# A four-layer graph network on one core: the last layer's attentions for two batches at once, with the own score as shift and the mask as a factor

## The chip, the cores and the metric

The kernel runs on one core of one Trainium2 chip. The metric is the device time of one execution in microseconds (us). Every kernel here was profiled once, and timed against runs of the kernel before in the same rounds on the same chip.

Engine names: PE is TensorE (matmuls), PEld its weight loads, DVE is VectorE, ACT ScalarE, POOL GpSimd. `L567` in a profile line is line 567 of that kernel's source; the numbers differ between kernels, so the text says what each line is.

## The reference, cut to what matters

Four graph layers over one adjacency matrix, each followed by a residual layer norm. Layers 0 to 2 are almost untouched by the change. Layer 3 is this:

```python
# x: [8, 2048, 64] float32; graph: [2048, 2048], ~0.4% ones, symmetric, ones on the diagonal
NEG = -1e+16
def _gat_layer(h, mask, b):
    scores = jnp.einsum('...nd,...md->...nm', h, h)
    scores = jnp.where(mask, scores, NEG)
    attn = jax.nn.softmax(scores, axis=-1)
    return jnp.einsum('...nm,...md->...nd', attn, h) + b
mask = graph + jnp.eye(N) > 0
h = jnp.einsum('bnc,hdc->bhnd', x, Wh)               # 4 heads of 64
out_h = _gat_layer(h, mask[None, None], bh[None, :, None, :])
cat = jnp.transpose(out_h, (0, 2, 1, 3)).reshape(B, N, H * D)
z = jax.nn.leaky_relu(cat, negative_slope=0.2)
h2 = jnp.einsum('bnk,dk->bnd', z, Wo)
out2 = _gat_layer(h2, mask[None], bo)                # the "second attention"
z2 = jax.nn.leaky_relu(out2, negative_slope=0.2)
out = layernorm(z2) * gamma + beta                   # then layernorm(x + out)
```

There are 8 batches with five attentions each (four heads and the second one), and each attention is a full 2048 x 2048 table of weights in fp32.

## The kernel before

Weights are made transposed: 128 source nodes on the partitions, 512 target nodes on the free axis. Such a block is called a **step**; 16 steps make a **chunk** of 512 targets, and 4 chunks an attention. For each attention `prepare` first finds the masked row maxima of the scores in bf16 (the shift of the softmax), and `attend` then makes weights and sums.

```python
def prepare(u, b, h):
    ...
        # 16 small products: h with nodes on partitions
        nc.tensor.matmul(ph[:, q], state["xT"][k * D:(k + 1) * D, ts],
                         WhT[k * D:(k + 1) * D, h * D:(h + 1) * D], start=True, stop=True)
    ...
    for it in range(NT):                 # row maxima, 64 blocks of 128 x 512
        for c in range(NCH):
            nc.tensor.matmul(pa, hb[:, it * P:(it + 1) * P], hb[:, cs], start=True, stop=False)
            nc.tensor.matmul(pa, neg_id_bf, M[:, it, cs], start=False, stop=True)
            nc.vector.tensor_reduce(mx[:, it, c:c + 1], pa, AX.X, ALU.max)
    ...                                  # maxima transposed into row 64 of hm

def attend(u, b, h):
    for c in range(NCH):
        for jt in range(NT):
            pscore = ps_s.tile([P, CW], F32, name="pscore")          # 3 buffers
            nc.tensor.matmul(pscore, neg_id_bf, MT[:, jt, cs], start=True, stop=False)   # the mask
            nc.tensor.matmul(pscore, hs[:, jt * P:(jt + 1) * P], hm[:, cs], start=False, stop=True)
            w = wk.tile([P, CW], F32, name="w", bufs=3)
            nc.scalar.activation(w, pscore, AF.Exp)
            nc.tensor.matmul(po, hones[...], w, start=(jt == 0), stop=(jt == NT - 1))  # [h | 1]
        rec = wk.tile([D, CW], F32, name="rec", bufs=1)
        nc.vector.reciprocal(rec, po[(1 - hk) * D:(2 - hk) * D])
        ...                              # times the numerators, bias, leaky relu, product with Wo
```

## Time and profile before

| | before |
|---|---|
| time | 9961.3 us (median of 3; 9961.0 to 9972.2) |
| layers 0 to 2 and set-up, to the first score of layer 3 | 2162 us |
| layer 3's attentions | 7769 us, TensorE busy 99% |
| one step (one batch) | 2.015 us, 2560 of them |

To read the profile: the page gives the busy time of each engine and, in 40 slices, its busy share in tenths. `PEclk` is the TensorE clock that the throttle granted, in tenths. A group line gives line, engine, operation, output <- input with shapes, count, then total busy us and the mean ns of one, then the idle time of the engine just before these instructions and what ended it. A timeline line gives start, time taken (us), engine, line, operation, output <- input, shapes, and how many records are merged in it (x4); in brackets stands the idle time before it. Matmuls overlap in the pipeline, so TensorE's pace is read from **starts** in the timeline, not from durations. A fp32 product appears as two matmul records, two **passes**. I call the 0.43 us between starts of two dense passes of 512 columns a **slot**.

### The profile page before, as it was taken

The numbers are of one execution on the slowest core, as the hardware profiler recorded it, in microseconds if no ns is written. First come the engines' busy times: TensorE is split into PE (matmuls) and PEld (weight loads), VectorE is DVE, ScalarE is ACT, GpSimd is POOL, SyncE is SP. The second block draws the span as 40 slices with busy tenths as digits, with TensorE's granted clock in tenths as the row PEclk, the third lists the DMA queues.
The fourth block names the chain that finished last, engine by engine and source line by source line (L and its number), as shares of the span: only waits on it lengthen the run. The fifth ranks groups of instructions, "written<-read, shape, count | busy, mean of one in ns | idle before, by whom it ended". The sixth has DMA issues, their size and how long they took to land. (4 is left out here: it accounts for less than half of the span.)

```text
span 9967.4 us, 62454 instructions
## 1 busy us (share of the span) xinstructions
PE 9215.5 (92%) x24992; PEld 3477.5 (35%) x24992; DVE 4228.1 (42%) x5463; ACT 1870.1 (19%) x3156; POOL 597.4 (6%) x471
## 2 busy tenths in 40 slices
PE   3786698679999999999999999999999999999998
PEld 2332244223333333333333333333333333333332
DVE  6899423454334333433443343334333433243423
ACT  1000200012212221222122212221222122212221
POOL 4100301310000000000000000000000000000000
PEclk6898799869989998999899989997999899989997
DMA  2000000000000000000000000000000000000000
GB/s 86 0 0 1 0 0 1 0 1 0 0 0 3 0 0 0 3 0 0 0 3 0 0 0 3 0 0 0 2 0 0 0 3 0 0 0 3 0 0 2
DMA packets 43381, 29.87 MB, mean 3 GB/s; under 512 B 40977, under 2 KB 41041, under 8 KB 41041
## 3 DMA queue, kind: packets, MB, share of 16 engines
q1 hardware_dynamic: 26448, 21.68, 0.7%
q10 hardware_dynamic: 16640, 4.20, 0.2%
q8 instruction: 195, 3.19, 0.1%
q14 instruction: 98, 0.79, 0.0%
HBM read 21.68 MB, written 4.19 MB: 3 GB/s over the span
## 5 line engine op out<-in xcount | busy, mean ns | idle before, releaser
L565 PE MATMUL po<-w,hones 128*128 128x512 f32 x5120 | 2656.5, 622 | 2.1 <-ACT w L564 2.1
L562 PE MATMUL pscore<-hm,hs 65*128 65x512 f32 x5120 | 2650.8, 598 | 0.0
L564 ACT ACTIVATE w<-pscore 128x512 f32<-128x512 f32 x2560 | 1528.6, 597 | 5867.9 <-PE pscore L562 5867.9
L542 DVE TENSOR_REDUCE mx<-pa 128x1 f32<-128x512 f32 x2560 | 1720.9, 691 | 1220.2 <-PE pa L541 1219.2
L567 DVE RECIPROCAL rec<-po 64x512 f32<-64x512 f32 x160 | 536.6, 3353 | 2864.2 <-PE po L565 2864.2
L565 PEld LDWEIGHTS po<-w,hones 128*128 128x128 f32 x5120 | 880.2, 191 | 1245.8 <-ACT w L564 1161.0
L562 PEld LDWEIGHTS pscore<-hm,hs 65*128 65x128 f32 x5120 | 984.7, 193 | 758.1 <-issue 630.7
L540 PE MATMUL pa<-hb 64*128 64x512 bf16 x2560 | 1119.5, 437 | 33.7 <-DVE hb L533 17.2
L541 PE MATMUL pa<-M,neg_id_bf 128*128 128x512 fp8e4 x2560 | 1126.7, 440 | 0.0
L561 PE MATMUL pscore<-MT,neg_id_bf 128*128 128x512 fp8e4 x2560 | 974.8, 382 | 0.2 <-ACT M L458 0.2
L540 PEld LDWEIGHTS <-hb 64*128 64x128 bf16 x2560 | 242.4, 95 | 1299.2 <-issue 1281.3
L270 PE MATMUL acc<-w,H 128*128 128x512 f32 x1024 | 489.1, 632 | 54.0 <-DVE w L267 53.2
L541 PEld LDWEIGHTS <-neg_id_bf 128*128 128x128 bf16 x2560 | 249.6, 97 | 738.6 <-issue 738.6
L534 POOL COPY hm<-hs 64x512 f32<-64x512 f32 x160 | 110.3, 691 | 6234.9 <-ACT hs L532 6234.9
L368 PE MATMUL pa<-R,A 128*128 128x512 f32 x1024 | 453.4, 599 | 9.7 <-POOL R L359 9.3
L561 PEld LDWEIGHTS <-neg_id_bf 128*128 128x128 bf16 x2560 | 249.1, 97 | 474.3 <-issue 469.1
L270 PEld LDWEIGHTS acc<-w,H 128*128 128x128 f32 x1024 | 198.7, 201 | 339.3 <-issue 204.3
L267 DVE SCALAR_TENSOR_TENSOR w<-MT,w 128x1024 f32<-128x1024 fp8e4 x256 | 302.1, 1215 | 0.4
L160 POOL TENSOR_TENSOR ln_rstd<-ln_var,mhalf 128x16 f32<-128x16 f32 (+1 forms) x21 | 151.0, 7189 | 2450.2 <-DVE ln_var L157 2450.2
L368 PEld LDWEIGHTS pa<-R,A 128*128 128x128 f32 x1024 | 191.3, 190 | 269.1 <-issue 245.9
L416 PE MATMUL pa<-Y,A 128*128 128x512 f32 x512 | 219.9, 592 | 0.0
L549 DVE COPY hm<-pm 1x512 f32<-1x512 f32 x160 | 109.0, 682 | 248.4 <-PE pm L548 248.4
(184 smaller groups left out, 3891.9 us busy)
## 6 DMA issues: line engine op xcount, KB each, us to landing
at<-in_adj SPq DMA_DIRECT2D x16, 1024.0 KB, 5.2
X<-in_x ACTq DMA_DIRECT2D x16, 256.0 KB, 7.8
out<-O SPq DMA_DIRECT2D x8, 512.0 KB, 3.8
wt<-in_L_gnn_Wh SPq DMA_DIRECT2D x4, 32.0 KB, 4.6
wo<-in_L_gnn_Wo SPq DMA_DIRECT2D x1, 64.0 KB, 6.0
a<-in_L_gnn_a SPq DMA_DIRECT2D x2, 32.0 KB, 2.9
g<-in_L_gnn_ln_gamma SPq DMA_DIRECT2D x2, 32.0 KB, 2.9
b<-in_L_gnn_ln_beta SPq DMA_DIRECT2D x2, 32.0 KB, 3.1
```

The lines of the kernel that those rows point to most:

```text
L267: nc.vector.scalar_tensor_tensor(w, MT[:, jt, ih * HW:(ih + 1) * HW], 0.0, w, op0=ALU.is_equal, op1=ALU.mult)
L270: nc.tensor.matmul(acc[c], H[:, jt, p, k:k + 2, :].rearrange("p a d -> p (a d)"), w[:, c * CW:(c + 1) * CW], start=(jt == 0), stop=False)
L368: nc.tensor.matmul(pof, A[:, jt], R[:, jt, h].rearrange("p a f -> p (a f)"), start=(jt == 0), stop=False)
L416: nc.tensor.matmul(po, A[:, jt], Y[:, jt], start=(jt == 0), stop=(jt == NT - 1))
L540: nc.tensor.matmul(pa, hb[:, it * P:(it + 1) * P], hb[:, cs], start=True, stop=False)
L541: nc.tensor.matmul(pa, neg_id_bf, M[:, it, cs], start=False, stop=True)
L542: nc.vector.tensor_reduce(mx[:, it, c:c + 1], pa, AX.X, ALU.max)
L561: nc.tensor.matmul(pscore, neg_id_bf, MT[:, jt, cs], start=True, stop=False)
L562: nc.tensor.matmul(pscore, hs[:, jt * P:(jt + 1) * P], hm[:, cs], start=False, stop=True)
L564: nc.scalar.activation(w, pscore, AF.Exp)
L565: nc.tensor.matmul(po, hones[:, jt, hp, hk:hk + 2, :].rearrange("p a d -> p (a d)"), w, start=(jt == 0), stop=(jt == NT - 1))
L567: nc.vector.reciprocal(rec, po[(1 - hk) * D:(2 - hk) * D])
```

## The change

Its intent is to make layer 3 cheaper in five ways at once:

- Two batches lie on the two halves of the partitions. A head's score products use 64 rows each and its sums 64 columns each, so the two batches' products can run on halves of the array at once.
- The shift of the softmax is the node's own score, not the row maximum: the pass of maxima falls away. The shift rides in the place of feature 0 of `U`.
- The mask is a factor (VectorE multiplies the weights by 0 or 1), not a product that adds minus infinity.
- Features of a layer-normed node add up to zero, so feature 0 is redundant in the heads. Its place in `Xo` holds ones, and the sums of the weights come out there: no separate ones. The second attention has no redundant feature and pays two more products with ones.
- If a denominator is out of range, a flag is set and the old layer 3 runs after all.

The core of the diff, with cuts marked (layers 0 and 1 only use the mask as a factor, or copy it, instead of comparing):

```diff
+    W_SELF = 20.0
+        ps_s = l3.enter_context(tc.tile_pool(name="f3pss", bufs=2, space=PSUM))
+        ps_o = l3.enter_context(tc.tile_pool(name="f3pso", bufs=2, space=PSUM))
+        ps_m = l3.enter_context(tc.tile_pool(name="f3psm", bufs=2, space=PSUM))
...
+        def prepare(p, h, c):
...
+            pu = misc([P, CW])
+            nc.tensor.matmul(pu, G[:, h], xT[:, cs], start=True, stop=True)
+            nc.scalar.copy(U[:, cs], pu)
+            V = wk.tile([P, CW], BF16, name="V")
+            nc.gpsimd.tensor_tensor(V, xT[:, cs], U[:, cs], ALU.mult)
+            pv = misc([P, CW])
+            nc.tensor.matmul(pv, minus, V, start=True, stop=True)
+            nc.vector.tensor_tensor(U[:, cs], pv, U[:, cs], ALU.add)
...
+        def attend(p, h, c):
...
+            for jt in range(NT):
+                pscore = ps_s.tile([P, 2, CW], F32, name="pscore")
+                for k in range(2):
+                    half = slice(k * D, (k + 1) * D)
+                    nc.tensor.matmul(pscore[:, k], left[half, jt * P:(jt + 1) * P], right[half, cs], start=True, stop=True)
+                w = wk.tile([P, 2, CW], F32, name="w", bufs=4)
+                nc.scalar.activation(w, pscore, AF.Exp, bias=bias)
+                edge = ET[:, jt, cs].unsqueeze(1).to_broadcast([P, 2, CW])
+                nc.vector.scalar_tensor_tensor(w, w, 3.0e38, edge, op0=ALU.min, op1=ALU.mult)
+                for k in range(2):
+                    half = slice(k * D, (k + 1) * D)
+                    nc.tensor.matmul(po[half], rhs[:, jt, k], w[:, k], start=(jt == 0), stop=(jt == NT - 1))
+                if h == HN:
+                    for k in range(2):
+                        half = slice(k * D, (k + 1) * D)
+                        nc.tensor.matmul(pden[half], ones_d, w[:, k], start=(jt == 0), stop=(jt == NT - 1))
...
+            if h < HN:
...
+                nc.scalar.copy(o, po)
...
+                nc.tensor.matmul(pden, first, o, start=True, stop=True)
...
+                nc.tensor.matmul(pn, AT[:, h], o, start=True, stop=True)
+                nc.vector.reciprocal(rec, pden)
+                nc.vector.tensor_tensor(z, pn, rec, ALU.mult)
...
+                nc.tensor.matmul(ph, WoT[:, h], z, start=True, stop=True)
...
+        bad = nc.values_load(flag[0:1, 0:1], min_val=0, max_val=P * NP * (HN + 1) * NCH)
+    with tc.If(bad > 0), ExitStack() as l3:
...      the old layer 3
```

A step of the new kernel covers two batches, so there are 1024 steps in heads and 256 in second attentions.

## The prediction

> **What bounds the kernel now.** I read the table of engines first, then the strip of slices, then the three stretches (layers 0 to 2, layer 3, the end), then the groups of instructions kept apart by shape, and last the timeline of six microseconds inside an attention.
>
> The page, busy time and the two rows of TensorE:
>
> ```profile
> PE 9215.5 (92%) x24992; PEld 3477.5 (35%) x24992; DVE 4228.1 (42%) x5463; ACT 1870.1 (19%) x3156; POOL 597.4 (6%) x471
> ...
> PE   3786698679999999999999999999999999999998
> ...
> PEclk6898799869989998999899989997999899989997
> ```
>
> TensorE is busy from slice 9 on and nothing else comes near. The small dips of its clock recur once per batch. The stretches say where layer 3 lies (columns: busy us and count of PE, PEld, DVE, ACT, POOL, then the granted clock):
>
> ```profile
> 0.00:2162.00 2162.00, 1533.96 (x4139) 686.59 (x4139) 1319.64 (x1591) 216.24 (x364) 382.38 (x259) 0.82 0.04 10
> 2162.00:9931.00 7769.00, 7679.74 (x20850) 2790.16 (x20848) 2894.16 (x3850) 1651.60 (x2788) 201.59 (x205) 0.94 0.00 1
> ```
>
> From the first score at 2162 us to the last weighted sum at 9931 us, 7769 us, TensorE is busy 99%. The change is almost wholly in that stretch. The groups say what it is made of:
>
> ```profile
> L565 PE MATMUL po<-w,hones 128*128 128x512 f32 x5120 | 2656.5, 622 | 2.1 <-ACT w L564 2.1
> L562 PE MATMUL pscore<-hm,hs 65*128 65x512 f32 x5120 | 2650.8, 598 | 0.0
> L564 ACT ACTIVATE w<-pscore 128x512 f32<-128x512 f32 x2560 | 1528.6, 597 | 5867.9 <-PE pscore L562 5867.9
> L542 DVE TENSOR_REDUCE mx<-pa 128x1 f32<-128x512 f32 x2560 | 1720.9, 691 | 1220.2 <-PE pa L541 1219.2
> L567 DVE RECIPROCAL rec<-po 64x512 f32<-64x512 f32 x160 | 536.6, 3353 | 2864.2 <-PE po L565 2864.2
> ```
>
> An fp32 product of 2560 is recorded as 5120 matmuls: two passes each. Durations of 600 ns overlap, so the pace must come from starts, which the timeline gives:
>
> ```profile
> 5240.43 0.38 PE L561 MATMUL pscore<-MT,neg_id_bf 128*128 128x512 fp8e4 x1
> ...
> 5240.65 1.02 PE L562 MATMUL pscore<-hm,hs 65*128 65x512 f32 x2
> ...
> 5241.51 2.03 PE L565 MATMUL po<-w,hones 128*128 128x512 f32 x4
> ...
> 5244.46 0.38 PE L561 MATMUL pscore<-MT,neg_id_bf 128*128 128x512 fp8e4 x1
> ```
>
> 5240.65 to 5241.51 is one fp32 product: 0.86 us, 0.43 a pass. The mask product is 0.22. Four passes of sums follow in a row, because the order takes two steps of scores and then two of sums. Two steps span 5240.43 to 5244.46, 4.03 us: **2.015 us a step** (one batch, one head, 128 sources, 512 targets). 2560 x 2.015 = 5158 us; the other 2611 us are the row maxima (2560 pairs of a bf16 and an fp8 product), and each unit's projections and ends.
>
> **What the Trainium skill says.** "FP8 and Floating Point Precision", TensorE Precision Notes: true fp32 takes four passes. The trace agrees in cost: 0.86 us against 0.22 for the fp8 product of as many columns. "TensorE: Matmul & The Clock Gate", Part 3, The mechanism: matmuls on different row groups or column groups run at once, but matmuls stay in strict order of issue. The kernel before never alternates tiles, so its trace cannot say; I lean on this most. "TensorEngine Tiling (Array Packing)", Key Properties: "Changing tiling mode (not just tile) drains the TensorE". The trace shows its price where the 64-row bf16 product of the maxima alternates with the 128-row one: 0.32 us from start to start against 0.22, so some 0.1 us for each switch, and more where an fp32 weight load (190 ns for 128 columns) can no longer hide. "VectorE: DVE Perf Modes", the section on the TRN2 errata: an fp32 two-tensor operation takes (N+151)/0.96 ns, 1224 for 1024 columns; the trace has 1215 for the one of layer 0 that multiplies 1024 weights by the fp8 mask.
>
> **The change, part by part.**
>
> Removed from layer 3: 2560 mask products of 0.22 (550 us); 2560 pairs for maxima, at 0.44 to 0.64 (1100 to 1600 us); the 1024 small fp32 projections with nodes on partitions, the 1280 small products that transpose the maxima (190 us), 2560 reductions on VectorE (1721 us, hidden). The second orientation of the mask goes too: about 100 us of the start, where layer 3 begins at about 2050 us after the last layer norm and scores only at 2162.
>
> Steps: 4 pairs x 5 attentions x 4 chunks x 16 = 1280, each for two batches, 1024 of them in heads, 256 in the second attention. A head's step has two fp32 score products on row halves, one exponential of 1024 columns, one multiplication by the mask, two fp32 sums on column halves. A second attention's step has two more sums with ones.
>
> ScalarE a step: 374 ns for 256 columns and 597 for 512 give 0.87 ns a column, so 1.05 us. VectorE: 1.215 us. TensorE, by order of issue: passes A1 A2 B1 B2; B1 can join A2, but not A1. So four passes take three slots of 0.43 = 1.29 us, not two. Where two steps stand together it is five slots, 2.15 for two. Mode switches, down and back with the first weight load exposed, I put at 0.5 us (estimate from the 0.1 and the 190 ns above). So a head's step costs 2 x 1.29 + 0.5 = 3.1 us if scores and sums alternate singly, and (2 x 2.15 + 0.5)/2 = 2.4 if they come two by two as before. I choose **2.75**, as exponential and mask now lie in series (1.05 + 1.215 us plus handovers) with two score buffers, so sums may wait some of the time: 1024 x 2.75 = 2816. A second attention's step: alternating 3 + 5 slots + 0.5 = 3.9; two by two (5 + 9) x 0.43 + 0.5 = 6.5, halved 3.3. I choose 3.7: 947 us.
>
> Work beside the steps on TensorE: in each of 64 head chunks one product for U (0.86), a bf16 one (0.3), three at the end (denominator, numerator, output projection: 2.6) and switches (0.5): 4.3 us, 275 in all. Transposes of inputs and outputs for four pairs: 40 us. VectorE at the end of each chunk: reciprocal 3.35, and four operations of about 0.69, some 6 us in which no mask is multiplied; buffers cover most, I take 2.5 us x 80 = 200. Sum for layer 3's steady part: 2816 + 947 + 275 + 40 + 200 = 4278.
>
> Before it: layers 0 to 2 keep their instructions in number and form (the mask is a factor instead of a comparison, the same two-tensor time on VectorE), so 2050 us, plus about 35 for loading the first pair and the first U: 2085. After it: 36 us before; now two batches' layer norm at once, the last second attention with nothing beside it, the flag and its branch: 60. Total 2085 + 4278 + 60 = 6423, rounded to **6400 us**.
>
> Does the old path run? I worked the reference's data through on the host. The test asks every denominator to lie between 1 and 2^115, whose logarithm is 79.7. In the heads the logarithms lie from 20.0 to 23.9; in the second attention, with its shift of 40 minus the mean squared norm (about 72), from 4.2 to 78.2. The margin above is only 1.5, but it holds: the old path is skipped.
>
> **Rivals.** (1) The halves don't overlap at all. Then a head's step is 8 passes of 0.43 plus 0.5 = 3.9 us, the second's 12 passes = 5.7: 1024 x 3.9 + 256 x 5.7 + 515 + 2145 = 8100 us. Nothing in the old trace speaks against it; the skill's measurements do. It would still win, by what it removes. 12%. (2) Alternating modes: every step pays two switches and never shares a slot with the next: 3.1 and 3.9 us give 3174 + 998 + 515 + 2145 = 6830. The two-by-two order before speaks against it, fewer score buffers (two instead of three) for it. (3) VectorE or the series of exponential and mask becomes the bound: VectorE's own work is 1.215 x 1280 = 1555 us, reciprocals 80 x 3.36 = 269, others about 250, so some 2070 of 4300; it can't bind on average, only by latency. If it bound each step, with slots hidden, layer 3 would be near 3300 and the total 5500. (4) The flag is set: 6400 + 7800 = 14200 us. 2%.
>
> **Range and chances.** Between full pairing at 2.3 us a step (about 5700) and a mix of alternation and stalls of 5 us a chunk (7100 to 7400) lie eight cases in ten: 5700 to 7400. Even without overlap it is faster by over 2%; slower needs the flag or a bound I don't see. Faster 0.96, same 0.01, slower 0.03.
>
> **What would show it.** Right: starts of a score's second half at about 0.43 us after the first half's, not 0.86; 2.4 to 3.1 us from step to step in heads; the exponential at about 1050 ns and the mask at about 1215; VectorE busy about half of layer 3; layer 3's scores beginning near 2085 us; no instruction of the old path. Wrong: second halves 0.86 us after the first (rival 1); gaps before sums that end with the mask's multiplication and make up over a fifth of the stretch (latency, my 2.75 too low); stalls at each chunk's end well over 2.5 us, with VectorE's reciprocal in them; a mask multiplication far off 1215 because GpSimd works at the same time.

## The result

The changed kernel is correct. It takes 5952.0 us (median of 4; 5944.3 to 5954.1) against 9961.2; the ratio is 0.597 (95% interval 0.596 to 0.598). Ratios here are the mean time of one kernel's runs over that of the other's of the same rounds, so not quite the ratio of the medians quoted. The forecast of 6400 had the direction right and was 450 us too high, inside its range.

The page of the changed kernel, engines and two rows of the strip (40 slices):

```profile
PE 4946.5 (83%) x15732; PEld 1612.3 (27%) x15732; DVE 3452.8 (58%) x3522; ACT 1631.7 (27%) x1844; POOL 585.1 (10%) x378
...
PE   4188883699797299999898999988899999899995
...
PEclk7599896799898599999998999999999999899998
```

TensorE is still the busiest by far, but no longer full: 8 and 9 alternate in layer 3. Its clock row is cleaner than before; that turns out to matter. The stretch of layer 3, columns as in the prediction (PE, PEld, DVE, ACT, POOL, granted clock):

```profile
2057.00:5884.00 3827.00, 3518.52 (x12011) 967.42 (x12009) 2174.81 (x1963) 1431.35 (x1509) 174.79 (x100) 0.98 0.01 1
```

It lasts 3827 us against 7769, and TensorE is busy 92% of it. The groups that answer to those of before:

```profile
L571 DVE SCALAR_TENSOR_TENSOR w<-w,ET 128x1024 f32<-128x1024 f32 x1280 | 1614.5, 1278 | 1433.8 <-ACT w L569 1433.8
L569 ACT ACTIVATE w<-pscore 128x1024 f32<-128x1024 f32 x1024 | 1034.0, 1023 | 1602.2 <-PE pscore L567 1602.2
L567 PE MATMUL pscore<-U,xT 64*128 64x512 f32 x4096 | 1295.7, 641 | 50.8 <-ACT w L569 50.8
L574 PE MATMUL po<-w,Xo 128*64 128x512 f32 x4096 | 1163.0, 626 | 146.7 <-DVE w L571 137.4
```

4096 score passes cost 1296 us of busy time, where 5120 of before cost 2651: 0.32 us a pass instead of 0.52. No instruction of the old path is in the trace. The timeline of a head:

```profile
3611.41 1.13 PE L567 MATMUL pscore<-U,xT 64*128 64x512 f32 x4
3612.48 1.08 PE L574 MATMUL po<-w,Xo 128*64 128x512 f32 x4
3613.49 1.13 PE L567 MATMUL pscore<-U,xT 64*128 64x512 f32 x4
3614.92 1.08 PE L574 MATMUL po<-w,Xo 128*64 128x512 f32 x4 [0.31 <-DVE w L571]
3615.93 1.13 PE L567 MATMUL pscore<-U,xT 64*128 64x512 f32 x4
```

This is the central reading. The four score passes of a step occupy TensorE for 3612.48 - 3611.41 = 1.07 us, and the four sums for 1.01. Two slots are 0.86, so both halves start together, twice, and the change from scores to sums costs 0.21 us, the one back 0.15. Single matmuls in the trace say the same; these are starts of the step of 3611.41:

```
scores  3611.407  3611.413     3611.940  3611.947
sums    3612.478  3612.484     3612.958  3612.964
```

Two passes start 6 ns apart and the next two 0.48 to 0.53 us later (the first slot after a change is longer than 0.43). From 3611.41 to 3615.93 are 4.52 us for two steps: **2.26 us a step**, of which 2.08 are TensorE's own and 0.18 (0.36 in every second step) a wait for the mask's multiplication.

### The profile page after: what moved, and what is told of

Read it like the earlier page. It is cut to its first block, busy times and chain, and to the rows that moved or that the text cites. A ratio compares the mean times of both kernels' runs of the same rounds, so it can differ in the third digit from the quotient of the medians.

```text
span 5942.5 us, 39158 instructions
## 1 busy us (share of the span) xinstructions
PE 4946.5 (83%) x15732; PEld 1612.3 (27%) x15732; DVE 3452.8 (58%) x3522; ACT 1631.7 (27%) x1844; POOL 585.1 (10%) x378
## 5 line engine op out<-in xcount | busy, mean ns | idle before, releaser
L571 DVE SCALAR_TENSOR_TENSOR w<-w,ET 128x1024 f32<-128x1024 f32 x1280 | 1614.5, 1278 | 1433.8 <-ACT w L569 1433.8
L569 ACT ACTIVATE w<-pscore 128x1024 f32<-128x1024 f32 x1024 | 1034.0, 1023 | 1602.2 <-PE pscore L567 1602.2
L567 PE MATMUL pscore<-U,xT 64*128 64x512 f32 x4096 | 1295.7, 641 | 50.8 <-ACT w L569 50.8
L574 PE MATMUL po<-w,Xo 128*64 128x512 f32 x4096 | 1163.0, 626 | 146.7 <-DVE w L571 137.4
L567 PEld LDWEIGHTS pscore<-U,xT 64*128 64x128 f32 x4096 | 364.9, 186 | 966.3 <-issue 548.0
L569 ACT ACTIVATE w<-pscore,shift 128x1024 f32<-128x1024 f32 x256 | 272.6, 1111 | 564.7 <-PE pscore L567 563.7
L567 PE MATMUL pscore<-h2T 64*128 64x512 f32 x1024 | 379.8, 631 | 43.9 <-ACT w L569 43.9
L574 PE MATMUL po<-w,H 128*64 128x512 f32 x1024 | 302.9, 610 | 16.9 <-DVE w L571 2.8
L265 DVE TENSOR_TENSOR w<-w,ET 128x1024 f32<-128x1024 f32 x256 | 302.0, 1214 | 0.4
L578 PE MATMUL po<-w,ones_d 128*64 128x512 f32 x1024 | 291.5, 595 | 0.0
L588 DVE RECIPROCAL rec<-pm 128x512 f32<-128x512 f32 x64 | 214.8, 3357 | 65.6 <-PE pm L585 65.6
```

The lines of the kernel that those rows point to most:

```text
L265: nc.vector.tensor_tensor(w, w, ET[:, jt, ih * HW:(ih + 1) * HW], ALU.mult)
L567: nc.tensor.matmul(pscore[:, k], left[half, jt * P:(jt + 1) * P], right[half, cs], start=True, stop=True)
L569: nc.scalar.activation(w, pscore, AF.Exp, bias=bias)
L571: nc.vector.scalar_tensor_tensor(w, w, 3.0e38, edge, op0=ALU.min, op1=ALU.mult)
L574: nc.tensor.matmul(po[half], rhs[:, jt, k], w[:, k], start=(jt == 0), stop=(jt == NT - 1))
L578: nc.tensor.matmul(pden[half], ones_d, w[:, k], start=(jt == 0), stop=(jt == NT - 1))
```

## The experiments

Experiments 1 to 3, 6 to 8 and 11 are built on the changed kernel without its flag and old path, which experiment 1 shows to be free. Experiments 4, 5 and 9 are built on the kernel before; 10 and 12 are the changed kernel with flag and old path. Groups of experiments ran on different chips, but the kernel before agrees within 0.3% between them (medians 9942 to 9966 us). The time of a kernel is the median of 4 runs; ratios are to the kernel before.

### 1. Without the flag and the old path

```diff
-        nc.vector.tensor_scalar(good, good, float(CW), None, op0=ALU.not_equal)
-        ...
-        bad = nc.values_load(flag[0:1, 0:1], ...)
-    with tc.If(bad > 0), ExitStack() as l3:
-        ...
```

> The changed kernel without the test of the denominators' flag and without the old path behind the branch. If the flag, its branch and the 22,000 instructions behind it cost only an end effect, the time falls by 5 to 25 us from 5952, all of it after the last store, and the pace of a head's chunk stays 43.0 us. Rival: the old path in the program slows the instruction stream or the placement of buffers; then the pace inside the chunks changes too and more than 60 us go. This kernel is also the base of the next ones.

Measured: 5952.6 us (5947.6 to 5953.4), ratio 0.598, correct. The flag and the branch over the old layer 3, which does not run, cost nothing that can be seen; my 5 to 25 us were too many.

### 2. Both score products on the same rows

```diff
-   nc.tensor.matmul(pscore[:, k], left[half, jt * P:(jt + 1) * P], right[half, cs], start=True, stop=True)
+   nc.tensor.matmul(pscore[:, k], left[0:D, jt * P:(jt + 1) * P], right[0:D, cs], start=True, stop=True)
```

The second batch of each pair then gets the first one's weights. Its output is wrong, which doesn't matter for the time. (The comparison passes all the same, I take it because with this data nearly all of a node's weight lies on the node itself. So "correct" in these experiments says little about small errors in the weights.)

> Wrong result on purpose: both score products of a step read partitions 0 to 63, so they use the same half of the array's rows; everything else as in e1. Theory (the two halves run at once, two slots of 0.43 us for four passes): the scores of a head's step grow from 1.07 to about 1.93 us, its wait for the mask vanishes, so a step goes from 2.26 to 2.94: 1024 x 0.68 = 700 us more, and some 60 us in the second attentions, about 6690. Rival (my forecast's three slots: first passes never overlap): about 0.43 us a step, of which the wait hides 0.18, 260 us, about 6200. Rival (no overlap at all, starts in the trace are only modelled): no change.

Measured: 6508.6 us, ratio 0.654, 556 more than experiment 1. The timeline of this kernel:

```profile
3613.54 1.98 PE L567 MATMUL pscore<-U,xT 64*128 64x512 f32 x4
3615.45 1.08 PE L574 MATMUL po<-w,Xo 128*64 128x512 f32 x4
3616.46 1.55 PE L567 MATMUL pscore<-U,xT 64*128 64x512 f32 x3
```

Scores now take 1.91 us, four slots of 0.43 and a change; sums are as before. The step is 2.92 us, as the theory said. A chunk of a head went from 43.0 to 51.7 us, 0.54 a step on average and not 0.66: steps within a chunk take 2.92 us throughout, and the rest is made up at the chunk's end, where scores and sums now stand in longer rows with less waiting. So the row halves run two at a time; without that the kernel is 556 us slower (about 740 were expected).

### 3. Both sums on the same columns

```diff
-   half = slice(k * D, (k + 1) * D)
+   kk = jt % 2 if h < HN and 2 <= jt < NT - 2 else k
+   half = slice(kk * D, (kk + 1) * D)
    nc.tensor.matmul(po[half], rhs[:, jt, k], w[:, k], start=(jt == 0), stop=(jt == NT - 1))
```

The result is wrong on purpose; a constant was added to the sums and Wo made smaller to keep it finite.

> Wrong result on purpose: in 12 of 16 steps of each head chunk both sums go to the same half of the columns; the second attention is left as it is. Theory (halves of the columns run at once too): 768 steps go from 2.26 to about 2.94 us, 520 us more, about 6450. Rival (columns don't overlap): no change.

Measured: 6583.1 us, ratio 0.662, 631 more than experiment 1 (about 500 were expected), and a head's chunk 53.6 us. The single starts of the sums of two steps, the first on the lower columns, the second on the upper:

```
lower columns  3631.195  3631.675  3632.104  3632.533
upper columns            3632.332  3632.812  3633.241  3633.670
```

Within one step the four passes now take four slots, so passes on the same columns do come one after the other. The second step's sums begin at 3632.33, when its mask's multiplication is done (3632.28), and before the last pass of the first step. The size of 631 is not clean, because the scheduler also took another order of steps for this kernel (two and two): I read the overlap from the starts and not from the total.

### 4. The old kernel with the own score as shift

```diff
-   for it in range(NT):
-       for c in range(NCH):
-           ...        # two products and a maximum for each block, and the mask's second orientation
+   for c in range(NCH):
+       nc.vector.tensor_tensor(sq, hs[0:D, cs], hs[0:D, cs], ALU.mult)
+       nc.tensor.matmul(pr, minus_col, sq, start=True, stop=True)
+       nc.vector.tensor_copy(hm[D:K1, cs], pr)
```

> The kernel before with one part of the change alone: the shift of a row is its own score, so the bf16 row maxima, their transposes and the second orientation of the mask go. One batch at a time, mask still by a matmul. From the trace of before: 2560 x 2.015 for the steps = 5158, 2070 before them, 480 for the small products, 160 for the new row of own scores, some 260 for ends and the waits before each second attention: about 8150 us. If the maxima had been hidden in waits, it would stay above 9000.

Measured: 8268.9 us, ratio 0.832, correct. The maxima with all that hangs on them were worth 1692 us of the 4009.

### 5. The same, with the mask as a factor

```diff
-   nc.tensor.matmul(pscore, neg_id_bf, MT[:, jt, cs], start=True, stop=False)
-   nc.tensor.matmul(pscore, hs[...], hm[:, cs], start=False, stop=True)
+   nc.tensor.matmul(pscore, hs[...], hm[:, cs], start=True, stop=True)
    nc.scalar.activation(w, pscore, AF.Exp)
+   nc.vector.scalar_tensor_tensor(w, MT[:, jt, cs], 0.0, w, op0=ALU.is_equal, op1=ALU.mult)
```

> e4 and one more part of the change: the mask is a factor on VectorE after the exponential, so the fp8 mask product of 0.22 us goes from each of 2560 steps. Still one batch at a time on the whole array. Theory: PE sets the pace, so 2560 x 0.22 = 563 us less than e4's 8269, about 7700; what is left to the changed kernel (5952) is then what the two batches at once give, some 1750. Rival: exponential (0.60) and multiplication (0.69) in series hold up the sums, as they do by 0.18 us a step in the changed kernel: then 7850 to 8100.

Measured: 8001.0 us, ratio 0.804, correct: 300 more than the theory said, and the number is the rival's. But not for the rival's reason. The timeline shows dense work, three steps of scores and three of sums in turn:

```profile
5022.63 2.74 PE L540 MATMUL pscore<-hm,hs 65*128 65x512 f32 x6
5025.20 2.74 PE L544 MATMUL po<-w,hones 128*128 128x512 f32 x6
5027.78 0.59 PE L540 MATMUL pscore<-hm,hs 65*128 65x512 f32 x1
```

5.15 us for three steps are 1.717 a step with no wait, 0.298 less than before, which over 2560 steps is 763 us. The kernel gained only 268. The rest is in the clock. Stretches of 10 us of TensorE (busy us, matmuls, granted clock, share of DMA, GB/s):

```profile
5210.00:5220.00 10.00, 10.00 (x24) 1.00 0.00 0
5220.00:5230.00 10.00, 10.00 (x42) 0.78 0.00 0
5230.00:5240.00 10.00, 10.00 (x12) 0.50 0.00 0
...
5260.00:5270.00 10.00, 10.00 (x12) 0.50 0.00 0
5270.00:5280.00 10.00, 10.00 (x21) 0.83 0.01 2
```

From 5220 to 5230 TensorE runs, among others, the small products that lay out the next head's h (32 passes of 64 columns). Within them the clock falls to 0.50 and stays there for some 45 us, although TensorE is busy all the time: 12 passes in 10 us instead of 24. (In these 45 us, steps alternate with products of 64 rows by 64 columns or by one column.) Before and after are at full clock. Adding up (1 - granted clock) over such stretches of layer 3 gives an estimate of the time lost: 456 us in the kernel before, 341 in experiment 4, **820 here**, and 70 in the changed kernel. The 479 us more than in experiment 4 account for 763 - 268 = 495. Bursts are not the only place where the clock falls. Of 38 falls in this kernel's layer 3, 26 begin within or right behind a burst, with no idle time of TensorE ahead of them (some 510 of the 820 us), the other 12 at or just after waits of 1.4 us or more; and in the kernel before, 340 of the 456 us are eight falls of 82 to 85 us that begin where TensorE has stood for 2 us ahead of a second attention, and last through its pass of maxima.

### 6, 7, 8. The order of the steps

The changed kernel leaves the order on TensorE to the scheduler. These three pin it: groups of `GROUP` steps of scores, then the sums that are over `LAG` steps behind.

```diff
+        GROUP, LAG = 1, 1     # experiment 6;  7: 1, 2;  8: 2, 2
+        def attend(p, h, c):
+            for jt in range(NT):
+                behind.append((p, h, c, jt, scores(p, h, c, jt)))
+                if jt % GROUP == GROUP - 1:
+                    drain(LAG)          # sums of the oldest, until LAG are left
```

> e1 with TensorE's order of the steps pinned: scores of step j, then sums of step j-1, halves always together. It is what the changed kernel does in most of a head's chunk, so it is the control for the next two. Heads: 2.26 us a step as now (order S, P, S, P with sums one step behind: 3.51 us from scores to sums against 3.15 of work between). Second attention: halves no longer split, 1.07 + 1.87 = 2.94 us a step instead of 3.585, 165 us less: about 5790. Rival: the splits cost nothing, no change.

Measured: 5837.5 us, ratio 0.586, a head's chunk 42.4 us; 115 less than experiment 1, where 165 were expected. The same order of steps as the scheduler's in heads, but the second attentions' pairs are no longer torn apart. In the changed kernel the scores of a second attention's two steps come in pieces, six passes and then, after a wait, the last two; a step takes 3.585 us:

```profile
5808.73 1.12 PE L567 MATMUL pscore<-h2T 64*128 64x512 f32 x2 [0.35 <-ACT w L569]
```

Pinned, a step takes 2.93 us, as the theory said (scores at 2930.36 and 2933.28). Yet a chunk of the second attention still takes 53 to 57 us, because sums at its end wait for the reciprocal, and the clock is at 0.50 for 3 to 14 us after that:

```profile
2972.35 1.08 PE L591 MATMUL po<-w,H 128*64 128x512 f32 x4 [2.82 <-DVE rec L623]
```

> Pinned order, sums two steps behind the scores. Theory (latency of exponential and mask, 0.36 us every second step): the waits before sums vanish, a head's step goes from 2.26 to the sum of its own work 2.08: 1024 x 0.18 = 184 us less than e6, about 5600. Rival (the 2.26 come from VectorE or ScalarE as engines): no change against e6.

Measured: 5645.5 us, ratio 0.567, chunk 39.9 us. With sums two steps behind, the wait for the mask is gone:

```profile
3600.90 1.13 PE L575 MATMUL pscore<-U,xT 64*128 64x512 f32 x4
3601.96 1.08 PE L591 MATMUL po<-w,Xo 128*64 128x512 f32 x4
3602.97 1.13 PE L575 MATMUL pscore<-U,xT 64*128 64x512 f32 x4
```

2.07 us from score to score, TensorE's own work and nothing else. This confirms that 0.18 us a step in the changed kernel is latency: from its scores' start to its sums' start a step needs 3.5 us (1.13 of scores, 1.02 of exponential, 1.23 of mask and the handovers), while one step behind offers 3.15 us of other work.

> Pinned order, two steps of scores, then two steps of sums, two steps behind: half as many changes between row halves and column halves. Theory (each change costs 0.1 to 0.2 us: 2.08 less 4 slots of 0.43 leaves 0.36 a step for two changes): a head's step (1.72 x 2 + 0.36)/2 = 1.90, a second attention's 2.76: 185 + 46 us less than e7, about 5370. Rival (the 0.36 are loads of weights or gaps between products, not the change of mode): as e7, 5600.

Measured: 5415.5 us (5413.3 to 5421.6), ratio 0.544, chunk 37.8 us:

```profile
3323.08 1.99 PE L575 MATMUL pscore<-U,xT 64*128 64x512 f32 x8
3325.00 1.94 PE L591 MATMUL po<-w,Xo 128*64 128x512 f32 x8
3326.87 1.99 PE L575 MATMUL pscore<-U,xT 64*128 64x512 f32 x8
```

Eight score passes take 1.92 us, four slots of 0.43 and 0.20; eight sums take 1.87, four slots and 0.15. So a change between row halves and column halves costs 0.15 to 0.2 us however long the groups are, and half as many changes make a step of 1.89 us.

### 9. The small products spread out

On experiment 5: one small product of the next head after every fourth step, pinned there, where the scheduler set 16 in a row.

```diff
+   i = nc.tensor.matmul(po, hones[...], w, start=(jt == 0), stop=(jt == NT - 1))
+   if nxt and nxt[1] < HN and jt % 4 == 3:
+       held = little(*nxt, c * 4 + jt // 4)     # one 64-column product
+       after(held, i)                           # and the next scores after it
```

> e5 with one thing moved: the 16 small products of each unit (128 outputs, 64 moving columns, fp32), which e5 does in two bursts of eight at the head of a unit, are pinned one after every fourth step. The work is the same, and so is the result. Theory: a burst of small products makes the throttle halve TensorE's clock, for some 40 us each time (e5: 1410 us of its layer 3 at 0.50, some 820 us lost by the sum of 1 less the clock; the clock falls 3 us into the burst); without bursts the time at half clock falls below 500 us and the time from 8001 to 7350 to 7650. Rival: the clock falls for the waits around a chunk's end or for the data; then the time at half clock stays above 1000 us and the time near 8000.

Measured: 8691.2 us, ratio 0.873, correct. A miss. Pinning broke the dense order of three and three: sums wait 1.41 us for the mask ahead of each small product. And the clock still fell at places (753 us lost by the same estimate, against 820): each of its 119 falls from 2200 us to the end of layer 3 has a wait of TensorE of 1.3 us or more in the 7 us before it. Of such waits there are 322 here and 22 in experiment 5, so the pinning took one occasion away and put another in its place. It can't tell whether the bursts of small products are what lowers the clock; that stays open.

### 10. The other products pinned as well

The changed kernel with its flag, the order of experiment 8, and the chunk's other products (denominator, numerator, U, own score, Wo) set between scores and sums of given groups.

```diff
+   if jt == 2 * GROUP - 1 and nxt:
+       later(0, lambda: prepare(*nxt, c))
+   run_due()
+   drain(LAG)
```

> The changed kernel whole, with its flag and old path, in the order of e8, and the other products of a chunk (U and own score for the next head, denominator, numerator, output projection) pinned too, between two steps of scores and two of sums. Theory: in e8 a head's chunk takes 37.8 us, of which 16 x 1.89 are steps and 7.5 the five other products, though these need 3.7 us of slots; the rest is halves of a pair torn apart and changes of mode. So 34.5 to 36 us a chunk, 64 x 2 to 3.3 us less than e8: 5210 to 5290. Rival: the 7.5 are VectorE's end of a chunk (reciprocal 3.36 us and more) holding up the masks; then pinning gains nothing or loses: 5400 to 5500.

Measured: 5426.3 us, ratio 0.545, correct, chunk 37.6 us: no gain over experiment 8. The rival, VectorE at the chunk's end, was right. The timelines of TensorE and of VectorE:

```profile
3331.37 1.12 PE L527 MATMUL pm<-xT,G 128*128 128x512 f32 x2 [2.88 <-DVE rec L655]
```

```profile
3327.96 3.35 DVE L655 RECIPROCAL rec<-pm 128x512 f32<-128x512 f32 x1
3331.23 1.16 DVE L585 SCALAR_TENSOR_TENSOR w<-w,ET 128x1024 f32<-128x1024 f32 x1
```

The product for U wants one of two buffers; both hold denominators and numerators until the reciprocal of 3.35 us is through. The mask of the next step stands behind the same reciprocal.

### 11. Lower, lower, upper, upper

Experiment 8, with the scores of two steps issued as lower rows of both steps first, then upper rows of both. If matmuls had to start in the order of issue, only the last of the lower could meet the first of the upper.

```diff
+   for k in range(2):
+       half = slice(k * D, (k + 1) * D)
+       for q in range(2):
+           pin(nc.tensor.matmul(state["ps"][q][:, k], left[half, ...], right[half, cs], ...))
```

> e8 with the four score products of two steps issued lower, lower, upper, upper half instead of lower, upper, lower, upper. Theory (products start in order of issue, whole fp32 products of two passes are the unit): the second lower must wait for the first, the first upper joins the second lower, so three slots of 0.86 us instead of two for two steps: 640 x 0.86 = 550 us more than e8, about 5965. Rival (each half has its own queue, order of issue is no matter): no change, 5415. Rival (order at the level of single passes, as in my forecast): then lower, upper, lower, upper would have cost three slots too, against what e8 shows.

Measured: 5508.1 us, ratio 0.554, 93 more than experiment 8, where order of issue would have cost about 550. The timeline, and below it the single starts of the eight score passes:

```profile
3600.36 1.99 PE L577 MATMUL pscore<-U,xT 64*128 64x512 f32 x8
3602.29 1.94 PE L595 MATMUL po<-w,Xo 128*64 128x512 f32 x8
```

```
3600.363  3600.376     3600.896  3600.910
3601.325  3601.339     3601.755  3601.768
```

Eight passes still take 1.93 us, in four pairs that start 13 ns apart. Products for the upper rows don't wait until the lower ones issued ahead of them have begun: each half moves on as if it had a queue of its own, as the columns did in experiment 3. (The trace doesn't name the half of a record; that the two of a pair lie on different halves is inferred from experiment 2, where passes on the same rows come one after the other.) That the products are issued as pinned shows where the product for the own score falls between the two lower ones and the two upper ones: there four passes on one half take 1.98 us, one after the other, twice.

```profile
3620.83 1.98 PE L577 MATMUL pscore<-U,xT 64*128 64x512 f32 x4
3622.91 0.38 PE L529 MATMUL pm<-V,minus 128*128 128x512 bf16 x1
3623.22 1.98 PE L577 MATMUL pscore<-U,xT 64*128 64x512 f32 x4
```

A chunk takes 39.3 us against 37.8, which makes up the 93 us. This place is the largest part of it: 4.3 us from these scores to their sums, where experiment 8 has 3.5.

### 12. The reciprocal in two halves, and U later

Experiment 10 with two edits that follow from its waits, made together, so what each is worth alone is not shown (a third number, `STAGE3`, went from 2 to 1 to make up for the group by which the second half is later):

```diff
-   if jt == 2 * GROUP - 1 and nxt:
+   if jt == 6 * GROUP - 1 and nxt:
        later(0, lambda: prepare(*nxt, c))
...
-   nc.vector.reciprocal(rec, pden)
+   nc.vector.reciprocal(rec[:, :half], pden[:, :half])
+   later(1, lambda: finish2b(p, h, c, rec, z, pn, pden))   # the other half, one group later
```

> The version with the flag and the old path of e10_best, with two edits: the product that makes U is moved from the second to the sixth group of steps of a chunk, so that it no longer asks for a buffer that the denominators and numerators still hold, and the reciprocal of 512 columns is taken in two halves, one in each of two groups, so that masks can pass between them. If the 2.88 us that TensorE stood before the U product in e10_best, and the masks held up behind the reciprocal, are what cost that version its gain, a head's chunk is eight groups of 3.785 us and 4.5 us of other products, about 34.8 us against 37.57, no wait over 1 us stands in it, and the time is 5200 to 5300 us (64 chunks by 2.8 us is 179 less than 5426). The rival, that the wait only moves on (VectorE's chunk end is as long as before, and the next product of the chunk or the scores wait instead), gives 37 us or more for a chunk and 5390 to 5440.

Measured: 5274.4 us (5270.0 to 5275.1), ratio 0.529 (0.528 to 0.530), correct, chunk 34.63 us where 34.8 was expected. A chunk's timeline has no wait left; for instance the product for U, which had waited 2.88 us:

```profile
3338.06 1.99 PE L581 MATMUL pscore<-U,xT 64*128 64x512 f32 x8
3339.98 1.13 PE L527 MATMUL pm<-xT,G 128*128 128x512 f32 x2
3341.03 1.94 PE L597 MATMUL po<-w,Xo 128*64 128x512 f32 x8
```

This version has the flag and the old path, and takes 678 us less than the changed kernel and 47% less than the one before.

| kernel | us | ratio | a head's chunk |
|---|---|---|---|
| before | 9961 | 1 | 32.2 for one batch |
| 4: own shift | 8269 | 0.832 | |
| 5: and mask as a factor | 8001 | 0.804 | |
| changed | 5952 | 0.597 | 43.0 for two batches |
| 2: same rows | 6509 | 0.654 | 51.7 |
| 6: one behind, pinned | 5837 | 0.586 | 42.4 |
| 7: two behind | 5645 | 0.567 | 39.9 |
| 8: two by two | 5415 | 0.544 | 37.8 |
| 12: and chunk ends pinned | 5274 | 0.529 | 34.6 |

(32.2 is 16 x 2.015.)

## Why the prediction was right or wrong

**The direction and the chances** were right, and for the reasons given: what the change removes was worth a great deal alone (experiment 4), and the halves do overlap (experiments 2 and 3), which excludes rival 1.

**The sum, term by term**, against the profiled run of 5942.5 us. The last column is the trace less the forecast.

| term | forecast | trace | difference |
|---|---|---|---|
| to the first score | 2085 | 2057 | -28 |
| heads' steps, 1024 | 2816 (2.75 each) | 2314 (2.26) | -502 |
| second attention's steps, 256 | 947 (3.7) | 918 (3.585) | -29 |
| rest of chunks: other products, VectorE at the end | 475 | 435 (64 x 6.8) | -40 |
| transposes; handovers to and from second attentions (what is left over) | 40 | 156 | +116 |
| after the last score | 60 | 63 | +3 |
| sum | 6423 | 5943 | -480 |

(6.8 is the chunk of 43.0 less 16 x 2.26. The forecast's 6423 was then rounded to 6400.)

**The step that failed is the head's step**, and in it one sentence: passes go "A1 A2 B1 B2; B1 can join A2, but not A1. So four passes take three slots". They take two. The trace has 1.07 and 1.01 us for four passes, two by two within 6 ns, and experiments 3 and 11 show that even an order that ought to set the halves apart does not: they don't wait for each other in the order of issue. With two slots in the place of three, the forecast's own sum would be 2 x 0.86 + 0.5 = 2.2 for steps that alternate singly, close to the 2.26 measured.

Two smaller terms of that step erred against each other. The two changes between rows and columns, 0.5 by estimate, are 0.36 us together. The wait for the mask's multiplication, which I had only hinted at in choosing 2.75, is 0.18 a step; experiment 7 takes it away.

**Order of the steps.** I had left open whether steps alternate singly or two by two. They alternate singly in heads, and for that order the forecast's own figure is 3.1 us a step (its rival 2, 6830 us in all). That the miss is 0.49 a step and not 0.84 is the luck of a choice between two orders. As for the other, experiment 8 gives what two by two is worth, 1.89 against 2.07 us.

**Second attention.** The 3.585 us for a step are near my 3.7, by luck: eight passes of sums need four slots and not five, and the scheduler tears pairs of scores apart and lets them wait. (Some 65 of the 115 us of experiment 6 lie in the second attentions, most of it in their first chunks, which go from 69 to 73 us to 57 to 60.)

**Handovers** around the second attentions were underestimated: from score to score, the first chunk of a second attention takes 69 to 73 us where the later ones take 56 to 57, and the first head's chunk after it 72 to 74 us, some 30 longer than the others.

**VectorE.** The mask's multiplication has a mean of 1278 ns, a twentieth over the 1215 I put down; exponentials are at 1023, where I had 1050. The flag stays down, as worked out. Two counts in the forecast are of passes and not of products (1024 small projections and 1280 small products are 512 and 640 fp32 products); the sum does not use them.

**What I had not foreseen: the clock.** In layer 3 the clock lost only 70 us instead of 456. This is part of the gain over the kernel before, though not of the error, since the forecast was built from full-speed slots. The whole gain is then: 1692 us by the maxima (experiment 4; 115 of it the clock's), 268 by the mask as a factor (experiment 5; 763 by its steps, less 479 by the clock), and 2049 by all that is left: the pairing above all, but also the small products that go with the old layout, which no experiment takes apart. In the last, steps went from 2560 x 1.717 = 4395 to 2314 + 918 = 3232 us, 1163 less, 750 is the clock, and some 136 is the rest. Why the clock falls is not shown: the traces have it fall within bursts of small products and near waits of TensorE of 1.3 us or more (experiments 5 and 9), and experiment 9, which should have tested the bursts, failed.

**Open:** the cause of the clock's fall; what the column halves alone are worth in time (experiment 3); what each edit of experiment 12 is worth.

## What to carry to other kernels

When two products use different halves of the array, count slots for each half by itself and pay 0.15 to 0.2 us here for each change between row halves and column halves; so put as many of one kind together as the score buffers allow. When exponential and mask lie in series, hold the sums far enough behind (two steps here) that the whole latency is covered by TensorE's other work, and pin the order where the scheduler tears pairs apart. A long VectorE operation at a chunk's end (a reciprocal) does its harm through the buffers it holds and the short operations behind it: split it, and move whatever asks for its buffers (experiment 12 did both at once).

## What the Trainium skill lacked or had wrong

- "TensorE: Matmul & The Clock Gate": Part 3, The mechanism, has matmuls start and end strictly in the order of the program. Issued lower, lower, upper, upper, eight fp32 passes still took 1.93 us, four slots of 0.43, where that order would need seven (experiment 11), and in experiment 3 a pass on the upper columns started 0.2 us before one on the lower columns of the step ahead. And by Part 1 the throttle lifts after about 3.4 us of sustained work; in experiment 5 the clock stayed at 0.50 for some 45 us with TensorE busy throughout, in part with products on a quarter of the array or less, 12 passes in 10 us instead of 24. (The caveats of the same part tell of a throttle that stuck for over 50 us, at another ratio.)
- "TensorEngine Tiling (Array Packing)", Key Properties, says that a change of mode drains TensorE, with no figure. The runs show 0.2 us from scores on row halves to sums on column halves and 0.15 back, the same for groups of four and of eight passes. Its other property, that tiles operate independently, agrees with experiment 11.
- I found no page with a duration for VectorE's reciprocal: 3357 ns for 512 columns and 1751 for 256 in fp32, nearly five times the 0.68 us of another fp32 operation on 512.
